# Convolution chain with a Haar layer: the filter networks on 128 partitions, two layers ahead of the first batch, the third inside it

## The chip, the cores and the metric

The kernel runs on one core of a Trainium2 chip (trn2). The metric is the device time in microseconds (us) of one execution. A core has a matrix engine (TensorE, PE in the profile, with its weight loads shown apart as PEld), a vector engine (VectorE, DVE), a scalar engine (ScalarE, ACT), GpSimd (POOL) and SyncE (SP); SP and ACT issue the DMAs here.

## The reference

The input x has 4 batches of 64 channels of 256 x 256 in float32. Four layers follow each other; layers 0, 1 and 3 are long convolutions, layer 2 works in a Haar basis.

```
def filter(z, w1, b1, w2, b2, w3, b3, wo, freq, t, deltas):   # for X and for Y
    h = sin(freq * (z @ w1 + b1)); h = sin(freq * (h @ w2 + b2)); h = sin(freq * (h @ w3 + b3))
    return (h @ wo) * exp(-t * abs(deltas))

# layers 0, 1, 3: k[c] = outer(hx[c], hy[c]); causal 2-d convolution, then the residual
y = irfft2(rfft2(x, 512x512) * rfft2(k, 512x512) / 512)[:256, :256] + x * bias

# layer 2: f = haar2d(x); f4 = conv_w[i] applied over channels to f * v[i]
#          acc += sign(f4) * relu(abs(f4) - tau[i]) for i = 0, 1;  y = haar2d_inverse(acc) + x
```

The kernel of each convolution is an outer product, so the convolution is a product with a triangular Toeplitz matrix along the rows and one along the columns. What the filter networks have to supply is one row of 256 numbers for each channel, axis (X or Y) and layer.

## The kernel before

**The filters (L55 to L138).** All inputs are loaded first. SP issues the Haar matrix `hbt`, `hrow`, the mixing weights `wb`, the biases `bsb`, the signs, the decay table `dsb`, and then for each of the three layers `z` (positions and first weights, 33 partitions) and `w` (the other weights, 64 partitions) (L63 to L93). ACT issues the Haar coefficients `vts` and their factors `fac` (L82 to L85). Then three steps run over the six pairs of a layer and an axis (L97 to L122). One step of one pair is one product of TensorE into 64 x 256 of PSUM (L103 or L105), eight operations of DVE on 64 partitions x 256 (L110 adds the bias and scales, L115 and L116 find the multiple of 2 pi, L118 takes it off in three pieces, L119 clamps) and one Sin on ACT (L121). A last product (L126) and one DVE operation with the decay (L129) give `f`, which L132 writes to the DRAM tensor `pad` of its layer. At the end DVE multiplies the coefficients by their factors (L134), and L135 writes them to the DRAM tensor `scales`.

**The stream of the convolutions.** `toeplitz` (L155 to L159) reads a channel's row from `pad` as 128 shifted copies, 256 KB for the two axes, into one of five buffers `t`. `first` and `second` do the two products of a convolution, each by `contract` (L164 to L168: two products of 256 columns and two of 128). ACT copies the result of the first (L176), DVE adds the residual to that of the second (L189). In batch 0, a channel passes these stages one tick after the other: load of `x` and of layer 0's `t`; `first` of layer 0; `second` of layer 0, which also issues the load of layer 1's `t`; `first` of layer 1; `second` of layer 1 with the first level of the Haar transform (L230, L231) and the write to `keep` (L232). Every four channels DVE does the other levels (L240, L241), and PE does one product each for the other direction (`down`, L259). Then come `mixing` (L284 to L349), which uses `scales` and `wb`, and `inverse` with layer 3's convolution. Batches overlap: the mixing of one runs beside the convolutions of the next.

**The order.** Each stage is put down by `at(tick, place, ...)`, and the list is worked off sorted by tick and place at the end of the function. That fixes the priority of the instructions, but not their order on an engine: a planner with its own cost model places each instruction on its engine's queue when its inputs and a buffer are ready by its reckoning, the lowest in the list first, and so lets later instructions move into gaps. The order on a queue is then fixed in the program, and each engine works its queue off in that order.

Of the kernel before, what the change touches and what calls it, by code (L numbers as in the profile page):

```python
# [9 lines left out]
F32 = mybir.dt.float32  # L10
F32R = mybir.dt.float32r
AF = mybir.ActivationFunctionType
ALU = mybir.AluOpType
PSUM = bass.MemoryType.PSUM
DRAM = bass.MemoryType.DRAM

B, C, S, EMB, ORD = 4, 64, 256, 33, 64
P = 128
ROW = S + P

GT = 8
BUFS = {"res": 1, "y": 3, "co": 2}

INV_2PI = float(np.float32(1.0 / (2.0 * math.pi)))
MAGIC = float(1.5 * 2.0**23)

C1 = 6.28125
C2 = 2028.0 / 2.0**20
C3 = float(np.float32(2.0 * math.pi - C1 - C2))
PI_IN = float(np.nextafter(np.float32(math.pi), np.float32(0)))  # L30


def ap(t, offset, dims):
    return bass.AP(tensor=t.tensor, offset=t.offset + offset, ap=dims)
# [3 lines left out]
def conv_seq_kernel(ctx, tc, x, fz, fw, bias, decay, haar, haar_row, factors, vt, taut, wmix, out):  # L38
# [14 lines left out]
    nc = tc.nc  # L53

    const = ctx.enter_context(tc.tile_pool(name="const", bufs=1))  # L55
    dram = ctx.enter_context(tc.tile_pool(name="dram", bufs=1, space=DRAM))


    hbt = const.tile([P, P], F32, name="hbt")
    hb = const.tile([P, P], F32R, name="hb")  # L60
    hbr = const.tile([P, P], F32R, name="hbr")
    hrow = const.tile([P, 2, P], F32, name="hrow")
    nc.sync.dma_start(hbt, haar[0])  # L63
    nc.sync.dma_start(hrow, haar_row)
    hsinv, ident = hrow[:, 0, :], hrow[:, 1, :]
    wb = const.tile([P, 2, P], F32, name="wb")
    nc.vector.memset(wb, 0.0)
    for r in range(2):
        nc.sync.dma_start(wb[r * C : (r + 1) * C, r, :], wmix)
    bsb = const.tile([P, 3, C], F32, name="bsb")  # L70
    nc.sync.dma_start(bsb, ap(bias, 0, [[0, P], [C, 3], [1, C]]))


    scales = dram.tile([S // 4 // GT, P, 2, GT, 16], F32, name="scales")
    pads = [dram.tile([C, 2, ROW], F32, name=f"pad{layer}") for layer in range(3)]
    with tc.tile_pool(name="filt", bufs=2) as fp, tc.tile_pool(name="fps", bufs=4, space=PSUM) as fps:
        signs = fp.tile([P, P], F32, name="signs", bufs=1)
        nc.sync.dma_start(signs, haar[1])
        nc.scalar.copy(hb, signs)
        nc.scalar.copy(hbr, hbt)  # L80
        vts = fp.tile([P, 2, S // 4, 16], F32, name="vts", bufs=1)
        nc.scalar.dma_start(vts[:, 0], vt)  # L82
        nc.scalar.dma_start(vts[:, 1], taut)
        fac = fp.tile([P, 2, S // 4, 16], F32, name="fac", bufs=1)
        nc.scalar.dma_start(fac, factors)  # L85
        dsb = fp.tile([C, S], F32, name="dsb", bufs=1)
        nc.sync.dma_start(dsb, decay)
        zs, ws = [], []
        for layer in range(3):
            z = fp.tile([EMB, S + 2 * ORD], F32, name=f"z{layer}", tag="z", bufs=3)  # L90
            nc.sync.dma_start(z, fz[layer])
            w = fp.tile([ORD, 2, 3 * ORD + 4], F32, name=f"w{layer}", tag="w", bufs=3)
            nc.sync.dma_start(w, fw[layer])  # L93
            zs.append(z)
            ws.append(w)
        cur = {}
        both = [(layer, axis) for layer in range(3) for axis in range(2)]  # L97
        for step in range(3):
            for layer, axis in both:
                z, w = zs[layer], ws[layer]  # L100
                ps = fps.tile([ORD, S], F32, name=f"fp{step}_{layer}_{axis}", tag="fps")
                if step == 0:
                    nc.tensor.matmul(ps, z[:, S + axis * ORD : S + (axis + 1) * ORD], z[:, :S], start=True, stop=True)  # L103
                else:
                    nc.tensor.matmul(  # L105
                        ps, w[:, axis, (step - 1) * ORD : step * ORD], cur[layer, axis], start=True, stop=True
                    )
                par = 3 * ORD
                u = fp.tile([ORD, S], F32, name=f"u{step}_{layer}_{axis}", tag="u", bufs=3)
                nc.vector.tensor_scalar(  # L110
                    u, ps, w[:, axis, par + step : par + step + 1], w[:, axis, par + 3 : par + 4], ALU.add, ALU.mult
                )

                k = fp.tile([ORD, S], F32, name=f"k{step}_{layer}_{axis}", tag="k", bufs=3)
                nc.vector.tensor_scalar(k, u, INV_2PI, MAGIC, ALU.mult, ALU.add)  # L115
                nc.vector.tensor_scalar(k, k, -MAGIC, None, ALU.add)  # L116
                for c in (C1, C2, C3):
                    nc.vector.scalar_tensor_tensor(u, k, -c, u, ALU.mult, ALU.add)  # L118
                nc.vector.tensor_scalar(u, u, PI_IN, -PI_IN, ALU.min, ALU.max)  # L119
                h = fp.tile([ORD, S], F32, name=f"h{step}_{layer}_{axis}", tag="h", bufs=12)  # L120
                nc.scalar.activation(h, u, AF.Sin)  # L121
                cur[layer, axis] = h  # L122
        for layer, axis in both:
            w = ws[layer]
            ps = fps.tile([C, S], F32, name=f"fo_{layer}_{axis}", tag="fps")
            nc.tensor.matmul(ps, w[:, axis, 2 * ORD : 3 * ORD], cur[layer, axis], start=True, stop=True)  # L126
            f = fp.tile([C, ROW], F32, name=f"f_{layer}_{axis}", tag="f")
            nc.vector.memset(f[:, S:], 0.0)
            nc.vector.scalar_tensor_tensor(  # L129
                f[:, :S], ps, 1.0 / (2 * S) if axis == 0 else 1.0, dsb, ALU.mult, ALU.mult  # L130
            )
            nc.sync.dma_start(pads[layer][:, axis, :], f)  # L132
        for i in range(2):
            nc.vector.tensor_mul(vts[:, i], vts[:, i], fac[:, i])  # L134
            nc.sync.dma_start(  # L135
                scales[:, :, i].rearrange("n p g j -> p n (g j)"), vts[:, i].rearrange("p (n g) j -> p n (g j)", g=GT)
            )


    zpool = ctx.enter_context(tc.tile_pool(name="zpool", bufs=1))  # L140
    tp = ctx.enter_context(tc.tile_pool(name="toep", bufs=5))
    io = ctx.enter_context(tc.tile_pool(name="io", bufs=2))
# [2 lines left out]
    psx = ctx.enter_context(tc.tile_pool(name="psx", bufs=2, space=PSUM))  # L145


    z = zpool.tile([P, 2, S, C], F32, name="z")

    sd = zpool.tile([P, 8, 2, 2, P], F32, name="sd")  # L150
    keep = [dram.tile([C, P, 2, 2, P], F32, name=f"keep{b}") for b in range(B)]
    coef = [dram.tile([2, C, P, S], F32, name=f"coef{b}") for b in range(B)]
    late = dram.tile([B, C, P, 2, S], F32, name="late")

    def toeplitz(layer, c, name):  # L155

        t = tp.tile([P, 2, S], F32, name=name, tag="toep")
        nc.sync.dma_start(t, ap(pads[layer], c * 2 * ROW, [[1, P], [ROW, 2], [1, S]]))
        return t  # L159
# [267 lines left out]


    put_off = range(2, C, 3)
    groups = S // 4  # L430
    ready = convolutions(0, range(C), in_parts=True)
    ahead = C
    start = ready + 3
    for b in range(B):
        mixing(b, start, 8 if b + 1 < B else 6)
        end = start + groups + 3
# [8 lines left out]
        start = max(end + C, ready + 3)  # L445
# [39 lines left out]
def _decay():  # L485
    t = np.linspace(0.0, 1.0, S)
    deltas = np.linspace(math.log(0.01) / 1.5, math.log(0.01) / 0.3, C)
    return np.exp(-t[None, :] * np.abs(deltas)[:, None]).astype(np.float32)[:, ::-1].copy()


# [68 lines left out]
```

## Time and profile before

| | us |
|---|---|
| median of 3 runs | 3088.14 |
| fastest and slowest of them | 3085.73, 3089.94 |
| the profiled execution | 3091.79 |
| its span in the profile | 3090.0 |

| stretch of the span | PE busy | DVE busy | ACT busy | DMA share |
|---|---|---|---|---|
| 8.30 to 57.57 us | 22.95 of 49.27 | 42.06 | 8.73 | 0.31 |
| 57.57 to 66.44 us | 8.18 of 8.87 | 0.75 | 0.59 | 0.54 |
| 66.44 to 345 us | 278.56 of 278.56 | 185.82 | 100.91 | 0.77 |

The profile shows one execution. Its page gives busy times of each engine over the whole span and in 40 slices; other views give the same for chosen stretches, the instructions in order of time (start, duration, engine, line, operation, output and input tiles, and in brackets the idle time before them and what ended it), and the waits by engine and line. PE counts as busy while a product is in its pipeline. The granted clock of TensorE is 1.00 in nearly all stretches.

### The profile page before, as it was taken

How to read it: one execution, taken by the hardware profiler on the slowest of the kernel's cores; microseconds unless marked ns; L12 is line 12 of the kernel's file. 1: busy time of each engine (PE TensorE's matmuls, PEld its weight loads, DVE VectorE, ACT ScalarE, POOL GpSimd, SP SyncE). 2: the span in 40 equal slices, each digit the busy share in tenths (PEclk: the TensorE clock that was granted, in tenths of full speed). 3: DMA queues.
4: the chain of work that ended last, by engine and by line, in shares of the span. 5: the costliest groups of instructions: out<-in, count | busy, mean ns of one | idle time of the engine just before them, and what ended most of it. 6: DMA issues, size and time to landing. Idle time of an engine off the chain costs nothing. (4 is left out here: it accounts for less than half of the span.)

```text
span 3090.0 us, 50474 instructions
## 1 busy us (share of the span) xinstructions
PE 3004.4 (97%) x16944; PEld 2615.3 (85%) x16944; DVE 2523.4 (82%) x4453; ACT 1926.9 (62%) x4054; POOL 0.2 (0%) x4
## 2 busy tenths in 40 slices
PE   5999999999999999999999999999999999999999
PEld 3999988888888888888887888888887888888998
DVE  6667677999987878888886879888886889998776
ACT  1333336777765656667665656666774667887554
POOL 0000000000000000000000000000000000000000
PEclk9999999999999999999999999999999999999999
DMA  4777877666667876666667776666667777877676
GB/s 118 217 230 230 234 227 211 196 193 197 195 193 228 238 223 196 195 207 199 194 205 216 236 229 196 199 195 204 198 195 218 235 238 228 236 233 212 210 211 188
DMA packets 555573, 649.26 MB, mean 210 GB/s; under 512 B 39761, under 2 KB 440500, under 8 KB 555188
## 3 DMA queue, kind: packets, MB, share of 16 engines
q1 hardware_dynamic: 439316, 493.18, 56.5%
q10 hardware_dynamic: 116000, 152.87, 13.7%
q8 instruction: 136, 2.23, 0.3%
q14 instruction: 121, 0.99, 0.1%
HBM read 426.40 MB, written 219.48 MB: 209 GB/s over the span
## 5 line engine op out<-in xcount | busy, mean ns | idle before, releaser
L167 PE MATMUL py<-t,a 128*128 128x256 f32 x3072 | 926.0, 383 | 27.9 <-ACT a L176 24.6
L176 ACT COPY a<-pa 128x512 f32<-128x512 f32 x768 | 458.7, 597 | 466.3 <-PE pa L168 330.7
L168 PEld LDWEIGHTS py<-t,a 128*128 128x128 f32 x3072 | 584.1, 190 | 79.4
L327 ACT ACTIVATE f<-px,vt 128x64 f32<-128x64 f32 x1920 | 422.0, 329 | 352.7 <-DVE f L325 348.3
L167 PEld LDWEIGHTS py<-t,a 128*128 128x128 f32 x3072 | 488.4, 191 | 126.1 <-issue 63.2
L168 PE MATMUL py<-t,a 128*128 128x128 f32 x3072 | 590.6, 274 | 0.0
L308 PE MATMUL px<-wb,f 128*128 128x256 f32 x2048 | 494.2, 380 | 4.3 <-ACT f L327 4.3
L308 PEld LDWEIGHTS px<-wb,f 128*128 128x128 f32 x2048 | 366.0, 191 | 44.1 <-ACT f L327 6.7
L335 DVE TENSOR_TENSOR mag<-mag,vt 128x1024 f32<-128x1024 f32 x256 | 312.2, 1219 | 36.0 <-ACT mag L333 34.8
L167 PE MATMUL pa<-t,x 128*128 128x256 f32 x1024 | 307.5, 382 | 9.4 <-DMA t<-pad 9.3
L340 DVE SCALAR_TENSOR_TENSOR mag<-mag,f 128x1024 f32<-128x1024 f32 x256 | 311.4, 1216 | 0.3
L167 PE MATMUL pa<-t,y 128*128 128x256 f32 x1024 | 306.3, 381 | 1.2 <-DVE y L189 0.9
L333 ACT ACTIVATE mag<-f 128x1024 f32<-128x1024 f32 x256 | 283.9, 1109 | 12.6 <-DVE z L344 6.8
L361 ACT COPY zc<-z 128x512 f32<-128x512 f32 x256 | 281.9, 1102 | 3.9 <-DVE z L199 2.6
L371 ACT CAST w<-pw 128x512 fp32r<-128x512 f32 x256 | 150.2, 587 | 212.3 <-PE pw L369 201.3
L334 ACT ACTIVATE f<-f 128x1024 f32<-128x1024 f32 x256 | 272.0, 1062 | 9.7 <-DVE sd L231 2.4
L189 DVE SCALAR_TENSOR_TENSOR y<-y,bsb,py 128x512 f32<-128x512 f32 x256 | 190.1, 743 | 104.5 <-PE py L168 103.7
L385 DVE SCALAR_TENSOR_TENSOR t<-r,pu 128x512 f32<-128x512 f32 x256 | 175.3, 685 | 86.6 <-PE pu L381 79.6
L189 DVE SCALAR_TENSOR_TENSOR y<-x,bsb,py 128x512 f32<-128x512 f32 x256 | 190.1, 743 | 62.6 <-PE py L168 54.0
L167 PE MATMUL pa<-t,u 128*128 128x256 f32 x772 | 234.1, 385 | 1.1 <-DVE y L189 0.7
L189 DVE SCALAR_TENSOR_TENSOR y<-u,bsb,py 128x512 f32<-128x512 f32 x193 | 143.8, 745 | 102.4 <-PE py L168 98.7
L168 PEld LDWEIGHTS pa<-t,x 128*128 128x128 f32 x1024 | 195.7, 191 | 26.9
(65 smaller groups left out, 4370.7 us busy)
## 6 DMA issues: line engine op xcount, KB each, us to landing
t<-pad SPq DMA_DIRECT2D x768, 256.0 KB, 3.9
x<-in_x SPq DMA_DIRECT2D x256, 256.0 KB, 3.9
keep<-sd ACTq DMA_DIRECT2D x256, 256.0 KB, 3.3
coef<-co SPq DMA_DIRECT2D x256, 256.0 KB, 3.1
f<-coef SPq DMA_DIRECT2D x256, 256.0 KB, 3.9
r<-keep SPq DMA_DIRECT2D x256, 256.0 KB, 3.4
out_y<-y ACTq DMA_DIRECT2D x256, 256.0 KB, 3.6
late<-u ACTq DMA_DIRECT2D x63, 256.0 KB, 2.6
```

The source lines that it names most:

```text
L167: nc.tensor.matmul(ps[:, m, :], src[:, 0, m * P : (m + 1) * P], t[:, ::-1], start=True, stop=False)
L168: nc.tensor.matmul(ps[:, m, P:], src[:, 1, m * P : (m + 1) * P], t[:, : P - 1 : -1], start=False, stop=True)
L176: nc.scalar.copy(a, ps)
L189: nc.vector.scalar_tensor_tensor(y, s[res], bsb[:, layer, c : c + 1], ps, ALU.mult, ALU.add)
L308: nc.tensor.matmul(ps[:, h, q, :], f[:, q, h * P : (h + 1) * P], wb.rearrange("p r n -> p (r n)"), start=True, stop=True,)
L327: nc.scalar.mul(f4[:, j], px[:, j], scale(g, 0)[:, j : j + 1])
L333: nc.scalar.activation(mag, f4, AF.Abs)
L334: nc.scalar.activation(f4, f4, AF.Sign)
L335: nc.vector.tensor_sub(mag, mag, over(g, 1, 16))
L340: nc.vector.scalar_tensor_tensor(mag, mag, 0.0, st[g]["f4"], ALU.max, ALU.mult)
L361: nc.scalar.copy(a, z[:, :, :, c].rearrange("p h (i k) -> p h k i", k=2))
L385: nc.vector.scalar_tensor_tensor(t, st[c]["r"], 0.5, ps, ALU.mult, ALU.add)
```

## The change

Four things change.

The whole block L59 to L138 goes; what it did is put elsewhere. The six pairs become three units: `filters(layer, queue)` works the X and the Y axis of one layer together on 128 partitions, with block diagonal weights made on the host (128 x 388 for one layer), so that one step is one product 128 x 256, eight DVE operations 128 x 256 and one Sin. The scale 1/512 of the X axis comes from a column of `dsb`. The two halves of `f` go to `pad` by two DMAs, on ACT's and on SP's queue.

Only layers 0 and 1 stand ahead of the convolutions, interleaved by hand, layer 0 first. The Haar constants (`constants`), layer 3's filter (`three`) and the coefficients (`tables`) are put into the list as stages of their own at place 3, the last place of a tick: constants at tick 4, layer 3's load at 7, its steps at 8 to 13, its end at 14, the load of the coefficients at 15 and the two scalings with their writes at 16 and 17. Their DMAs are on SP's queue, but for one half of `f`.

`warm(n)` adds products without use: 128 x 256, from `f` on itself into a PSUM tile nobody reads, six after layer 0's end and nine after layer 1's end.

All work tiles of the filters lie in the space of `z` (128 KB on each partition), which the kernel first writes in the mixing of batch 0. The coefficients lie over layer 0's and layer 1's inputs and over part of layer 3's.

```
...
-        both = [(layer, axis) for layer in range(3) for axis in range(2)]
-        for step in range(3):
-            for layer, axis in both:
...
+    room = z.rearrange("p h r c -> p (h r c)")
+    def filters(layer, queue):
+        fz_sb, fw_sb = part(S + P, EMB), part(3 * P + 4)
...
+        def load():
+            nc.sync.dma_start(fz_sb, fz[layer])
+            queue.dma_start(fw_sb, fw[layer])
+        def begin(n):
+            ps = bank(f"fp{layer}_{n}").rearrange("p m s -> p (m s)")[:, :S]
...
+            u, k = st["u"], st["k"] = part(S), part(S)
...
+            nc.vector.tensor_scalar(k, k, -MAGIC, None, ALU.add)
+        def finish(n):
+            u, k, h = st["u"], st["k"], part(S)
+            for c in (C1, C2, C3):
+                nc.vector.scalar_tensor_tensor(u, k, -c, u, ALU.mult, ALU.add)
+            nc.vector.tensor_scalar(u, u, PI_IN, -PI_IN, ALU.min, ALU.max)
+            nc.scalar.activation(h, u, AF.Sin)
...
+        def end():
...
+            nc.tensor.matmul(ps, fw_sb[:, 2 * P : 3 * P], st["h"], start=True, stop=True)
+            nc.vector.scalar_tensor_tensor(f[:, :S], ps, dsb[:, S:], dsb[:, :S], ALU.mult, ALU.mult)
+            for axis, queue in enumerate((nc.scalar, nc.sync)):
+                queue.dma_start(pads[layer][:, axis, :], f[axis * C : (axis + 1) * C])
+        def warm(n):
+            ps = psx.tile([P, 2, S], F32, name=f"warm{layer}", tag="mix")
+            for i in range(n):
+                nc.tensor.matmul(ps[:, i % 2, :], st["f"][:, :P], st["f"][:, :S], start=True, stop=True)
+        steps = [(lambda n=n, do=do: do(n)) for n in range(3) for do in (begin, finish)]
+        return [load, *steps, end, warm]
...
+    def tables():
...
+        def load():
+            nc.sync.dma_start(vts[:, 0], vt)
+            nc.sync.dma_start(vts[:, 1], taut)
+            nc.sync.dma_start(fac, factors)
...
+    one, two, three = filters(0, nc.scalar), filters(1, nc.scalar), filters(2, nc.sync)
+    one[0]()
+    nc.sync.dma_start(dsb, decay)
+    two[0]()
+    nc.sync.dma_start(bsb, ap(bias, 0, [[0, P], [C, 3], [1, C]]))
+    for do in (one[1], one[2], two[1], one[3], one[4], two[2], one[5], one[6], two[3], one[7], *two[4:7]):
+        do()
+    one[8](6)
+    two[7]()
+    two[8](9)
+    for tick, do in enumerate([constants, None, None, *three[:-1], *tables()], 4):
+        if do is not None:
+            at(tick, 3, lambda unit, do=do: do(), 0)
```

## The prediction

> **What bounds the kernel now.** I read the page first (busy shares, 40 slices), then the busy times by stretches of 10 us, the instructions in order of time up to 80 us, and last the waits and the DMA issues.
>
> ```profile
> PE 3004.4 (97%) x16944; PEld 2615.3 (85%) x16944; DVE 2523.4 (82%) x4453; ACT 1926.9 (62%) x4054; POOL 0.2 (0%) x4
> ...
> PE   5999999999999999999999999999999999999999
> ```
>
> TensorE is full in all slices but the first, so the gap to look into is there. The stretches (length, then PE, PEld, DVE, ACT, POOL busy, granted clock, DMA share, GB/s):
>
> ```profile
> 40.00:50.00 10.00, 4.87 (x11) 1.42 (x10) 10.00 (x30) 1.67 (x4) 0.00 (x0) 1.00 0.12 29
> 50.00:60.00 10.00, 2.41 (x7) 2.08 (x8) 1.57 (x7) 0.00 (x0) 0.00 (x0) 1.00 0.90 245
> 60.00:70.00 10.00, 9.33 (x40) 8.03 (x39) 1.37 (x2) 1.76 (x3) 0.00 (x0) 1.00 0.38 102
> 70.00:80.00 10.00, 10.00 (x62) 9.19 (x62) 4.03 (x9) 2.35 (x4) 0.00 (x0) 1.00 0.67 188
> ```
>
> Up to 47 us DVE is the bound (10.00 of 10.00), then DMA (0.90), then PE for good. The instructions (start, duration, engine, line, operation):
>
> ```profile
> 8.33 5.38 PE L103 MATMUL fp<-z 33*64 33x256 f32 x12 [8.33 <-DMA z<-in_fz]
> 8.73 2.22 SPq L221 DMA_DIRECT2D x<-in_x  x4
> 9.48 0.53 DVE L110 TENSOR_SCALAR u<-fp,w 64x256 f32<-64x256 f32 x1 [8.08 <-PE fp L103]
> ...
> 13.38 0.42 ACT L121 ACTIVATE h<-u 64x256 f32<-64x256 f32 x1 [3.85 <-DVE u L119]
> 14.21 0.29 PEld L105 LDWEIGHTS fp<-h,w 64*64 64x64 f32 x2 [1.33 <-ACT h L121]
> ...
> 46.64 0.41 DVE L129 SCALAR_TENSOR_TENSOR f<-fo,dsb 64x256 f32<-64x256 f32 x1
> 47.08 1.12 SPq L132 DMA_DIRECT2D pad<-f  x2
> 48.74 1.51 SPq L135 DMA_DIRECT2D scales<-vts  x2
> 52.64 1.09 SPq L158 DMA_DIRECT2D t<-pad  x2
> 53.97 0.34 SPq L294 DMA_DIRECT2D vt<-scales  x1
> 57.59 1.19 PE L167 MATMUL pa<-t,x 128*128 128x256 f32 x2 [8.46 <-DMA t<-pad]
> 61.16 1.22 PE L167 MATMUL py<-t,a 128*128 128x256 f32 x2 [0.67 <-ACT a L176]
> 66.44 0.71 PE L167 MATMUL pa<-t,y 128*128 128x256 f32 x2
> ```
>
> The first convolution starts at 57.59. Three contractions run until 66.44 (those starting at 57.59, 61.16 and 63.88), each some 2.55 us; from 66.44 on one takes 1.31 (the next start at 67.76 and 69.07). So the state at 66.44 is that of a start at full speed at 66.44 - 3 x 1.31 = 62.5. I use the event "first product of layer 1 (`pa<-t,y`)" as the marker: from 66.44 to 345 us PE is busy 278.56 of 278.56, so whatever moves this event moves the batch.
>
> **What the skill says.** (1) The Trainium skill, "VectorE: DVE Perf Modes", section "The TRN2 errata": an fp32 tensor_tensor costs (N+151)/0.96 ns, N being the elements on a partition; partitions don't enter. For N = 256 that is 424 ns; L230 on 128 x 256 shows 424, L118 on 64 x 256 shows 409. (2) "TensorE: Matmul & The Clock Gate", Part 1: a cold array runs at half rate until about 3.4 us of sustained activity. The trace agrees with the half (2.55 against 1.31), though the switch came 8.8 us after 57.59 with a wait of 0.67 between, and the granted clock says 1.00 all along. (3) "DMA: Bandwidth & Descriptors", "Queues, rings and completion order": what one engine issues goes through its own rings in order, on the same 16 DMA engines as the other's. So a large load on SP delays the `t` behind it; the 256 KB `t` take 3.9 us in the median of the run and 4.8 between 40 and 70 us, beside the `scales`.
>
> **The change, part by part** (all against the span of 3090.0 us).
>
> Start. `z` is issued at 5.08 on SP, behind seven other DMAs, and used at 8.33: 3.25 us. Issued first, at 0.73, it is used at 3.98. `w` goes on ACT's queue at 0.73; its 198 KB against 98 (2.8 us to landing) may bring it 1 us later, still before DVE asks for it at 5.1. One table load of 1.28 us is hidden in that wait.
>
> DVE. In place of 18 rounds of eight operations there are 6 before the convolutions, at the same duration each (1). A lone round: product to DVE 1.15 (8.33 to 9.48); 0.53 + 3 x 0.28 + 3 x 0.41 = 2.60, with 0.03 between dependent operations 2.75; Sin 0.42; ACT to the next weight load 0.41 (13.80 to 14.21): 4.75 in all. Layer 0: 3.98 + 3 x 4.75 + 1.15 + 0.41 = 19.8 for its `f`, where before had the first at 47.05. The last rounds of layer 1 lie behind: its second round's DVE part starts after layer 0's third (17.4), ends with layer 0's end between at 20.6; two passes through ACT and PE (1.98 each), one DVE part and the end give 27.7. The work tiles start at odd element offsets in `z`; if that cost the three SBUF-only operations their 0.28 against 0.41, it would be 0.13 x 9 = 1.2 on this path. Nothing shows it: bound 0 to 1.2, I take 0.
>
> To the convolutions. Layer 1's `pad` lands 3.0 us after 27.7 (median), its `t` 3.9 later: 34.6. PE: six products without use fill gaps after 20; the nine stand after 27.7. A 256-column product is a third of a contraction: 0.85 cold, 0.44 warm, so they end between 31.7 and 35.4. The three contractions after them take 3.9 warm and 0.7 to 1 of waiting for ACT, as at 60.5. The marker falls at 36.4 to 40.2, later than the `t` needs; I take 37.8. **Gain: 66.44 - 37.8 = 28.6**, bounds 26 to 32 (32 if the planner lets the contractions run ahead of the nine, and the `t` at 34.6 decides).
>
> Layer 3, constants. PE: four products at 0.44 = 1.75 when among the convolutions, nothing if the planner pulls them ahead as it pulled the four `x` loads (8.73) and a `vt` (53.97): 1.0, bounds 0 to 1.75. DVE: three rounds at 2.06 (half the 4.13 from 13.61 to 17.74 for two), an end, 2 x 1.2 for the coefficients: 9 us, in a stretch where DVE has a third free. What queues behind them on DVE is the residual `y` (L189), for which PE waits two contractions later (2.6 us, less 0.75): a round's second half (1.5) just fits. On ACT three Sin and two casts, 1.9 us, in front of the copies that PE awaits, with about as much room. If these pieces are pulled forward they sit between layer 1's rounds instead. Cost 1.0, bounds 0 to 3.
>
> Coefficients. 2 MB of loads and 1 MB of writes, formerly beside the filters (first 10 us) and beside `pad` and `t` (48 to 57), go to SP's queue among the convolutions, where DMA is 0.77 busy. Six `t` are wanted at once and there are five buffers, so a `t` is issued when PE frees one. Layer 1's is freed one contraction into a tick (1.31), lands 3.9 later (5.2) and is needed one contraction into the next tick (4 x 1.31 + 1.31 = 6.55): room 1.3 us, and the same for layer 0's. Behind 1.5 to 2 MB at the 290 GB/s reached around 53 us a `t` loses 5 to 7 us; behind a 512 KB write 1.8. Stall: from 0 (pulled to where PE waits anyway, or split by the planner) to (7 - 1.3) + 2 x (1.8 + 1.2 - 1.3) = 9. I take 4.
>
> Sum: 28.6 - 1.0 - 1.0 - 4.0 = 22.6. The profiled execution (3091.79, span 3090.0) lies 3.7 above the median of 3088.14; I take the gain off the median: **3065.5**.
>
> **Rivals.**
> A. The coefficients are free: they move under layer 1's wait, where DMA was 0.00 to 0.12 busy in the filter stage. For it: the planner does pull loads ahead. Against: they lie over layer 3's inputs. Gain 28.6 less 0 to 2, a little more if their DMAs leave `pad` and `t` alone: some 29, 3059.
> B. SP stands still: scaling and write follow the load on SP's queue, and every `t` behind waits for DVE. Load 7, multiply 1.2, twice a write 1.8, 1.2 more: 13 less 1.3; 28.6 - 2 - 12 = 14.6, 3073.5. For it: SP's waits for buffers, 949 us on L158 in total.
> C. Slower: the eleven stages at ticks 4 to 17 each hold PE, because the planner puts a DMA or a round in front of the `t` or the `y` that PE wants next. At 4 us a stage it is 44 - 28.6 = +15, 3103.5; it decides from 28.6/11 = 2.6 a stage. Against it: room of 1.3 to 1.9 us each.
> D. The useless products don't hold the clock: the wait between them and layer 1's `t` is long enough for a cold start. Three contractions at 2.55 in place of 1.31: 3.7, so 3069. It lies within my forecast's range.
>
> **How the numbers follow.** Forecast with D 0.60 (3060 to 3071), A 0.15, B 0.17, C 0.04; 0.04 for a loss elsewhere (the mixing stages replanned) that eats the gain without more. The range takes in A and B but for their outer parts: 3055 to 3080. Faster by over 0.2% (6.2 us, about what a measurement of this kernel can tell from no change): 0.92; within: 0.04; slower: 0.04.
>
> **What would show it.** First filter product near 4.0; first `f` near 19.8, layer 1's near 27.7; contractions of 1.31 from their start; `pa<-t,y` near 37.8. Waits of PE for `t<-pad` behind the coefficients' loads, some 4 us in all, tell forecast from A and B. A marker after 42, or PE idle over 10 us between it and 345 - 28 us, would make it wrong; so would mixing stages that differ from before by more than the shift.

## The result and the profile after

| | before | after |
|---|---|---|
| median of 4 runs each | 3086.93 us | 3070.60 us |
| fastest and slowest | 3083.40, 3089.94 | 3068.05, 3078.94 |
| span of the profiled execution | 3090.0 | 3066.3 |
| ratio after to before | | 0.9952, 95% interval 0.9930 to 0.9974 |

The changed kernel is faster by 16.3 us between the medians (8 to 22 by the interval) and by 23.7 between the two profiled spans. A second, larger set of runs of the same kernel (the first experiment) gave 18.4 us, ratio 0.9941 with an interval of 0.9928 to 0.9953. The forecast was 22.6 us, to 3065.5.

The top of the page of the changed kernel (busy us, share, instructions; then tenths busy in 40 slices):

```profile
PE 2998.0 (98%) x16950; PEld 2618.5 (85%) x16950; DVE 2505.8 (82%) x4384; ACT 1919.6 (63%) x4044; POOL 0.2 (0%) x4
...
PE   7999999999999999999999999999999999999999
```

Only the first slice has changed, from 5 to 7: most of what is gained lies in the first 77 us. The busy times of its first stretches (length, PE, PEld, DVE, ACT, POOL, granted clock, DMA share, GB/s):

```profile
10.00:20.00 10.00, 2.94 (x6) 1.32 (x5) 6.81 (x21) 1.23 (x4) 0.00 (x0) 1.00 0.06 20
...
40.00:50.00 10.00, 10.00 (x63) 9.23 (x62) 4.29 (x8) 2.34 (x4) 0.00 (x0) 1.00 0.60 180
...
60.00:70.00 10.00, 9.88 (x57) 8.55 (x56) 6.11 (x12) 1.82 (x4) 0.00 (x0) 1.00 0.55 170
```

While the filters of layers 0 and 1 run, DVE no longer fills a stretch (6.81 of 10.00 where it was 10.00 up to 47 us). PE fills the stretch from 40 us on, where before the first full one began at 70. But in the last line PE has 9.88, and from 110 to 120 us only 8.05, where before it never left 10.00 from 70 us on. The instructions in order of time:

```profile
3.17 1.22 PE L109 MATMUL fp<-z 33*128 33x256 f32 x2 [3.17 <-DMA z<-in_fz]
...
9.64 1.22 PE L111 MATMUL fp<-z 128*128 128x256 f32 x2 [3.57 <-ACT z L125]
14.33 2.08 PE L111 MATMUL fp<-z 128*128 128x256 f32 x4 [3.46 <-ACT z L125]
20.52 1.22 PE L130 MATMUL fo<-z 128*128 128x256 f32 x2 [4.11 <-ACT z L125]
21.78 0.48 DVE L133 SCALAR_TENSOR_TENSOR z<-fo,z 128x256 f32<-128x256 f32 x1 [1.56 <-PE fo L130]
22.38 4.70 PE L142 MATMUL warm<-z 128*128 128x256 f32 x12
27.55 0.49 DVE L133 SCALAR_TENSOR_TENSOR z<-fo,z 128x256 f32<-128x256 f32 x1 [1.29 <-PE fo L130]
28.09 4.15 PE L142 MATMUL warm<-z 128*128 128x256 f32 x18 [0.58 <-DVE z L133]
32.08 0.59 PE L189 MATMUL pa<-t,x 128*128 128x256 f32 x2
32.51 0.38 PE L190 MATMUL pa<-t,x 128*128 128x128 f32 x2
...
36.95 0.60 PE L189 MATMUL pa<-t,y 128*128 128x256 f32 x2
```

Layer 0's filter is there at 22.26 (start and duration of the first L133), layer 1's at 28.04. The first convolution stands directly behind the nine useless products of 28.09, with no wait of its own. The marker `pa<-t,y` falls at 36.95 in place of 66.44: 29.5 us. Not all of it is kept. PE's two largest waits in the 110 us behind the marker (total us, times, longest), of 3.7 us in all, where before had none:

```profile
PE pa L189 <- DMA t<-pad: 1.5, 1, 1.5
PE pa L189 <- DVE y L211: 1.2, 3, 0.5
```

**A second ruler.** DVE adds the residual 768 times (L189 before, L211 after), in the same order in all kernels, so the start of the same residual in two profiles says by how much one kernel is ahead there. At the 49th residual (200.43 and 178.74 us, when layer 3's filter and the coefficients are done) the changed kernel is 21.7 us ahead, at the last one 24.1. So the loss behind the marker is 29.5 - 21.7 = 7.8 us; a further gain of 2.4 comes much later. All kernels on this ruler:

| kernel | marker at | ahead at the marker | ahead at residual 49 | loss between | ahead at the last | median of the times |
|---|---|---|---|---|---|---|
| before | 66.44 | 0 | 0 | 0 | 0 | 3086.9 to 3088.6 |
| after | 36.95 | 29.5 | 21.7 | 7.8 | 24.1 | 3070.6 |
| after, repeated | 36.73 | 29.7 | 24.2 | 5.5 | 19.6 | 3070.2 |
| no useless products | 35.62 | 30.8 | 25.0 | 5.9 | 27.2 | 3064.6 |
| six useless products only | 34.30 | 32.1 | 25.1 | 7.1 | 35.4 | 3054.2 |
| coefficients apart | 38.52 | 27.9 | 25.9 | 2.0 | 23.1 | 3067.4 |
| all three layers first | 42.87 | 23.6 | 23.6 | 0.0 | 22.5 | 3069.9 |
| coefficients in pieces | 37.06 | 29.4 | 25.8 | 3.6 | 30.4 | 3061.9 |
| 64 partitions | 54.28 | 12.2 | 2.1 | 10.1 | 11.2 | 3080.5 |
| layers in turn | 38.65 | 27.8 | 20.5 | 7.3 | 29.4 | 3062.8 |
| in turn, eight useless products | 35.11 to 35.22 | 31.2 to 31.3 | 24.5 to 25.0 | 6.2 to 6.8 | 32.0 to 35.1 | 3055.1, 3059.3, 3057.2 |
| the same, coefficients in pieces | 33.54 | 32.9 | 26.4 | 6.5 | 37.2 | 3053.6 |

The columns up to the residual 49 can be followed in the trace. What lies between it and the last residual is a subject of its own, at the end of the next section.

### The profile page after: what moved, and what is told of

It is laid out like the page before. It is cut to its first block, busy times and chain, and to the rows that moved or that the text cites. A ratio compares the mean times of both kernels' runs of the same rounds, so it can differ in the third digit from the quotient of the medians.

```text
span 3066.3 us, 50357 instructions
## 1 busy us (share of the span) xinstructions
PE 2998.0 (98%) x16950; PEld 2618.5 (85%) x16950; DVE 2505.8 (82%) x4384; ACT 1919.6 (63%) x4044; POOL 0.2 (0%) x4
## 5 line engine op out<-in xcount | busy, mean ns | idle before, releaser
L189 PE MATMUL py<-t,a 128*128 128x256 f32 x3072 | 925.5, 383 | 30.4 <-ACT a L198 26.2
L189 PEld LDWEIGHTS py<-t,a 128*128 128x128 f32 x3072 | 488.1, 191 | 128.7 <-issue 64.0
L189 PE MATMUL pa<-t,y 128*128 128x256 f32 x1024 | 306.9, 381 | 2.7 <-DVE y L211 2.3
L189 PE MATMUL pa<-t,x 128*128 128x256 f32 x1024 | 305.8, 380 | 1.7 <-DMA t<-pad 1.5
L356 ACT ACTIVATE f<-f 128x1024 f32<-128x1024 f32 x256 | 272.1, 1063 | 10.1 <-DVE sd L253 3.7
L211 DVE SCALAR_TENSOR_TENSOR y<-y,bsb,py 128x512 f32<-128x512 f32 x256 | 190.3, 743 | 101.8 <-PE py L190 101.0
L211 DVE SCALAR_TENSOR_TENSOR y<-x,bsb,py 128x512 f32<-128x512 f32 x256 | 190.4, 744 | 57.7 <-PE py L190 49.3
L189 PE MATMUL pa<-t,u 128*128 128x256 f32 x772 | 234.4, 385 | 0.6 <-DVE u L411 0.5
L211 DVE SCALAR_TENSOR_TENSOR y<-u,bsb,py 128x512 f32<-128x512 f32 x193 | 143.9, 746 | 99.8 <-PE py L190 98.1
L262 DVE TENSOR_TENSOR sd<-sd 128x512 f32<-128x512 f32 (+6 forms) x448 | 164.3, 367 | 65.8 <-DMA keep<-sd 38.0
```

What stands on the lines that cost most here:

```text
L189: nc.tensor.matmul(ps[:, m, :], src[:, 0, m * P : (m + 1) * P], t[:, ::-1], start=True, stop=False)
L211: nc.vector.scalar_tensor_tensor(y, s[res], bsb[:, layer, c : c + 1], ps, ALU.mult, ALU.add)
L356: nc.scalar.activation(f4, f4, AF.Sign)
```

## The experiments

My theory after the result was: of the 7.8 us lost behind the marker, the coefficients' DMAs take the larger part and layer 3's four products the rest; and the nine useless products stand in front of the convolutions rather than help them. The rivals: the overlap of batches was planned anew and costs something; layer 3's rounds on DVE delay the residuals; without useless products three contractions run cold.

**1. The changed kernel once more.**

> The changed kernel once more, to narrow its ratio. If the single profiled execution tells the gain (span 3066.3 against 3090.0, 23.7 us), the ratio comes near 0.992; if the four runs' medians do (3070.6 against 3086.9, 16.3 us), near 0.995. First product of layer 1 at 37.0 us, PE idle some 3.7 us between 57 and 147 us.

Measured: 3070.18 us (3066.94 to 3072.86), span 3070.7. The ratio of 0.9941 lies between the two cases, nearer to that of the medians. The marker is at 36.73, so the start repeats to 0.2 us; the loss up to residual 49 is 5.5 in place of 7.8, and PE waits 2.2 us in the 110 us behind the marker, not 3.7. A single profile therefore fixes the cost behind the marker only to some 2 us.

**2. No useless products.**

```diff
-    one[8](6)
     two[7]()
-    two[8](9)
```

> The changed kernel without the fifteen products without use. If they earn their place: the first convolution starts about 2.5 us earlier (29.5) but cold, three contractions of 2.55 us, first product of layer 1 near 38.2, so 1 us slower than the changed kernel. Rival, the nine only hold the convolutions back: contractions are at 1.31 us soon, first product of layer 1 near 34.5, 2.5 us faster.

Measured: 3064.59 us, ratio 0.9921 (0.9908 to 0.9935), faster than the changed kernel beside it (experiment 1) by 5.6. The instructions in order of time:

```profile
29.32 1.19 PE L189 MATMUL pa<-t,x 128*128 128x256 f32 x2 [2.12 <-issue]
...
30.73 1.06 PE L189 MATMUL pa<-t,x 128*128 128x256 f32 x2
...
32.90 0.70 PE L189 MATMUL py<-t,a 128*128 128x256 f32 x2 [0.68 <-ACT a L198]
```

The first `t` is used at 29.32, 2.8 us ahead of the 32.08 above. Only the first contraction is cold (1.06 where 0.60 is full rate), the second is already at full rate at 32.90. So the fifteen useless products as they stand lose 1.3 us at the marker; 35.62 is nearer to the rival's 34.5 than to 38.2. In the two traces, PE's order differs by these fifteen products alone, and DVE's (4384 instructions) and SP's not at all; on ACT only a few neighbours change places. Against the kernel before, the orders on PE, DVE and SP differ only in the filters and the first part of batch 0. The rival of batches planned anew is refuted by that.

**3. The coefficients in a stretch of `z` of their own**, so that nothing holds back their loads.

```diff
-        free[0] = S + 1
+        free[0] = 16384
...
+        free[0] = S + 1 + 4096
```

> The coefficients lie in a stretch of their own in z, so that nothing holds their loads back and the planner can pull them ahead of the convolutions; all else as changed. Theory, their loads behind tick 15 cost the 1.5 us wait of PE for the t and about 0.7 us of waits for y: PE idle between 57 and 147 us falls from 3.7 to about 1.5, first product of layer 1 stays at 37 to 38, span 2 us shorter. Rival, their 3 MB only move the stall: in front of the first pads and t, first product of layer 1 at 40 or later, span equal or longer.

Measured: 3067.4 us, ratio 0.9930 (0.9917 to 0.9942). PE has no wait at all in the 110 us behind the marker, and the loss is 2.0. Layer 3's filter still runs among the convolutions here: it costs its products and next to nothing else. The coefficients, then, cost 5.8 us in the profile of the result and 3.5 in its repetition, if layer 3 costs the same in all three. But the marker is at 38.52. In order of time:

```profile
21.55 1.51 SPq L172 DMA_DIRECT2D scales<-z  x2
...
26.94 0.81 SPq L317 DMA_DIRECT2D vt<-scales  x2
...
29.26 8.50 SPq L181 DMA_DIRECT2D t<-pad  x6
33.55 0.70 PE L190 MATMUL pa<-t,x 128*128 128x256 f32 x2 [0.68 <-DMA t<-pad]
```

The pulled-forward writes of `scales` and the reads of `vt` stand in front of `pad` and `t` on SP, and the first `t` is issued at 29.26 where the changed kernel issues it at 26.06. So 1.6 us of the cost has moved in front of the marker (1.8 against the repetition). At residual 49 this kernel is still 1.7 to 4.2 us ahead of the changed one, and in the median 2.8 us ahead of the one beside it, where the intervals of the ratio overlap. What was measured lies between theory and rival.

**4. All three layers in turn ahead of the convolutions**, coefficients apart as in 3.

```diff
+    three[0]()
...
-    for do in (one[1], one[2], two[1], one[3], one[4], two[2], one[5], one[6], two[3], one[7], *two[4:7]):
-        do()
-    one[8](6)
+    for step in range(1, 7):
+        for layer in (one, two, three):
+            layer[step]()
+    one[7]()
     two[7]()
+    three[7]()
+    one[8](6)
     two[8](9)
...
```

> As tables_apart, and all three layers' filters ahead of the convolutions, step by step in turn. Theory, the gain comes from the 128 partitions and from the gaps in DVE that a third chain fills: nine rounds at 2.06 us end near 25.5, layer 1's pad leaves near 26 to 28 as in the changed kernel, first product of layer 1 near 37.5, and behind it PE has no idle time and no products of layer 3 (5.4 us less), span near 3061. Rival, moving layer 3 behind is what gains: with it ahead the first product of layer 1 comes at 37 + 3 x 2.06 = 43 and the span is 3067 to 3070.

Measured: 3069.85 us, ratio 0.9938 (0.9924 to 0.9951). The loss behind the marker is nil, as it must be with nothing left there, but the marker is 5.4 us later than my theory had it, and where the rival had it (42.87 for 43; the span of 3067.9 is in its range too):

```profile
19.33 8.50 SPq L173 DMA_DIRECT2D scales<-z  x2
...
28.19 3.95 SPq L135 DMA_DIRECT2D pad<-z  x3
30.94 7.22 PE L142 MATMUL warm<-z 128*128 128x256 f32 x26
...
32.87 2.47 SPq L182 DMA_DIRECT2D t<-pad  x5
38.00 0.59 PE L191 MATMUL pa<-t,x 128*128 128x256 f32 x2
```

Layer 0's filter, in turn with two others, ends 5.9 us later than in the changed kernel (28.17). Three `pad` writes on SP take until 32.1, so the first `t` is issued at 32.87, and thirteen useless products keep PE until 38.0. Against experiment 3 the marker is 4.4 us later and the loss 2.0 smaller: at residual 49 it is worth 2.3 us to have layer 3 behind the convolutions' start. The times say the same (2.5 us), with intervals that overlap.

**5. Units of 64 partitions again**, everything else as in the changed kernel (two layers first, useless products, layer 3 in the ticks). Each axis is a unit with its own tiles:

```diff
-        fz_sb, fw_sb = part(S + P, EMB), part(3 * P + 4)
+        fz_sb, fws = part(S + P, EMB), [part(3 * P + 4, C) for _ in range(2)]
...
+        units = [unit(axis) for axis in range(2)]
         def begin(n):
+            for u in units:
+                u[0](n)
```

> The changed kernel with its filters back on 64 partitions, one unit for each axis; order, placing and useless products as changed. Theory: DVE then has twelve rounds of 2.06 us ahead of the convolutions, 4.4 + 24.7 + 2.4 = 31.5 for layer 1's last f in place of 27.6, first product of layer 1 near 41; four products of layer 3 more among the convolutions (1.75 us); span 6 to 8 us longer than the changed kernel. Rival, the 128 partitions are most of the gain: each of six more rounds counts in full, first product of layer 1 at 37 + 12.4 = 49, span 14 us longer.

Measured: 3080.51 us over 9 runs, ratio 0.9976 (0.9966 to 0.9985). The marker is at 54.28, where my theory had 41 and its rival 49: both too early. In order of time:

```profile
37.37 1.22 PE L210 MATMUL pa<-t,x 128*128 128x256 f32 x2
37.48 0.42 DVE L136 SCALAR_TENSOR_TENSOR z<-fo,z 64x256 f32<-64x256 f32 x1 [0.44 <-PE fo L133]
38.52 8.05 PE L163 MATMUL warm<-z 64*128 64x256 f32 x18
46.50 0.80 PE L211 MATMUL pa<-t,x 128*128 128x128 f32 x2
...
54.28 0.60 PE L210 MATMUL pa<-t,y 128*128 128x256 f32 x2
```

Layer 1's filter ends at 37.90, 9.9 us behind the changed kernel: that is what the 128 partitions give to the filters themselves. Another 3.9 us is the nine useless products, which take 8.05 in place of 4.15: they run cold. They stand between the first product of layer 0's first convolution and the rest of it. And from 46.50 to the marker it takes 7.8 us, where the changed kernel takes 4.4 from the same product (32.51): the contractions are cold too. 9.9 + 3.9 + 3.4 = 17.2 of the 17.3 us at the marker. Of the 29.5 us, then, 12.2 come with all the rest of the change at the old width (two layers in place of three, their order, the start of the loads), and 17.3 with the width and what follows from it.

**6. The coefficients in eight pieces**, stages at ticks 15 to 30, each loading or scaling one eighth.

```diff
-        def load():
-            nc.sync.dma_start(vts[:, 0], vt)
...
+        def load(n):
+            g = slice(n * GT, (n + 1) * GT)
+            nc.sync.dma_start(vts[:, 0, g], vt[:, g])
...
+        def scale(n):
...
+            nc.vector.tensor_mul(vts[:, :, g], vts[:, :, g], fac[:, :, g])
+            nc.sync.dma_start(scales[n], vts[:, :, g])
```

> The changed kernel with the coefficients loaded, scaled and written in eight pieces (256 KB in, 128 KB out), still in the stages from tick 15 on. Theory, a single large load in front of a t on SP's rings is what PE waits for: PE idle in the 110 us behind the first product of layer 1 falls from 2.2 to 3.7 to under 1, first product of layer 1 stays near 37, span 2 to 3 us shorter. Rival, the bytes count and not their grouping: the same idle time, spread over more ticks.

Measured: 3061.9 us, ratio 0.9918 (0.9905 to 0.9932). The marker is unchanged (37.06), and the loss behind it is 3.6 us in place of 5.5 and 7.8. All waits of PE in the 110 us behind the marker:

```profile
PE pa L189 <- DVE y L211: 0.8, 1, 0.8
PE pz L281 <- DVE y L211: 0.3, 1, 0.3
```

No wait for `t` is left. That repeats: the changed kernel and experiments 1, 2, 7, 8, 9, 11 and 12, all with whole tables, have one such wait each, of 1.5 to 2.2 us, and the two kernels with pieces (6 and 10) have none. So large transfers in front of a `t` make PE wait for it, and small ones don't. That pieces lower the whole loss is not shown: 3.6 is within some 2 us of 5.5, and experiment 10 has no smaller loss than its kernel with whole tables.

**7. and 8. Layers 0 and 1 step by step in turn**, without useless products and with eight of them behind both ends.

```diff
-    for do in (one[1], one[2], two[1], one[3], one[4], two[2], one[5], one[6], two[3], one[7], *two[4:7]):
-        do()
-    one[8](6)
-    two[7]()
-    two[8](9)
+    for step in range(1, 8):
+        one[step]()
+        two[step]()
+    one[8](8)
```

(The last line is in experiment 8 alone.)

> No useless products, and the first two layers step by step in turn in place of layer 0 first. Theory, layer 1's second product stands behind layer 0's third on PE and its chain leaves DVE idle; in turn both are done near 22.5 us (21.8 and 27.6 before). The first convolution still starts near 29.3 behind layer 0's pad and t, one contraction runs cold: first product of layer 1 near 35.6, as in no_warm. Rival: layer 1's t was what it waited for, and it comes 5 us earlier, near 31.

> As turns, with eight products without use behind both layers' last products, in the 7 us in which PE waits for pad and t. Theory: they end before 29.3, hold nothing back, and all three contractions run at 1.31: first product of layer 1 near 33.9, 1.7 us before turns. Rival: as in the changed kernel they end later than the t lands, or the clock falls back before the convolutions: 35.6 or later.

Measured: 3062.77 us without (ratio 0.9920, 0.9907 to 0.9934) and 3055.1 with the eight (0.9896, 0.9882 to 0.9909). In order of time behind the two filters, first without, then with:

```profile
29.89 1.19 PE L189 MATMUL pa<-t,x 128*128 128x256 f32 x2 [6.92 <-DMA t<-pad]
...
37.47 1.06 PE L189 MATMUL pa<-t,x 128*128 128x256 f32 x2
...
38.65 0.60 PE L189 MATMUL pa<-t,y 128*128 128x256 f32 x2
```

```profile
22.72 5.34 PE L142 MATMUL warm<-z 128*128 128x256 f32 x16
30.13 0.70 PE L189 MATMUL pa<-t,x 128*128 128x256 f32 x2 [2.08 <-DMA t<-pad]
...
35.11 0.60 PE L189 MATMUL pa<-t,y 128*128 128x256 f32 x2
```

In turn, both filters end by 23.5, so the second is there 4.5 us sooner than in the changed kernel. The first `t` comes to PE no sooner (29.89), since layer 0's filter ends no sooner (22.64 against 22.26). Without useless products all three contractions are cold, until 38.5, where I had expected one and the marker at 35.6. The eight useless products end 2.1 us ahead of the first `t`, delay nothing, and the convolutions start at full rate: the marker is 3.5 us earlier, though 1.2 later than the theory's 33.9. Useless products do what they are meant to do where they end before the data is there.

**9. and 10. Kernel 8 again, and kernel 8 with the coefficients in pieces** (the edits of 8 and 6 together).

> The kernel with the two layers in turn and eight useless products, once more, on the chip and in the call of the next one. If its 3055.1 us belong to the program and not to the call, it is within 4 us of that, the marker at 35.1 within 0.3, PE idle in the 110 us after it 3 us. If a good part of its gain over the changed kernel (15 us in the times against 2 us at the marker) was luck with the half-rate windows of TensorE's clock, it falls between 3060 and 3066.

> The two layers in turn, eight useless products, and the coefficients in eight pieces instead of three whole tables. Theory (the 3 us of PE idle in the first batch come from the large DMAs of the coefficients alone, and add to the rest): marker 35 as without the pieces, idle after it at most 1, the time 2 to 3 us under that of the kernel with whole tables in this call. Rival (pieces pulled forward stand in front of layer 1's pads and their copies on SP): marker 36.5 or later, and no difference in the time.

Measured: 3059.29 us (0.9916, 0.9902 to 0.9929) and 3053.60 (0.9889, 0.9875 to 0.9902). The times differ by 5.7, more than I expected, but the trace gives only part of that: the marker is 1.6 us earlier (33.54), and the loss behind it is the same 6.2 to 6.5, with another cause: there is no wait for `t` any more, but 3.0 us of waits for the residual on DVE. So the theory was right on the waits for `t` and wrong on what is left without them; the 3059.3 lies just outside the 4 us that I had allowed it and under the 3060 of the other case.

**11. and 12. Six useless products only, and kernel 8 a third time beside it.**

```diff
     one[8](6)
     two[7]()
-    two[8](9)
```

> As the changed kernel, without the nine useless products behind layer 1's end; the six behind layer 0's end stay. Theory (the six alone bring the clock up, since they and layer 1's last product end 2 us before the first t has landed; the nine only stand in front of the convolutions): first convolution at 29.3 as without useless products, at 0.44 us a product and not 0.85, marker at 33.9 to 34.5 if layer 1's t (issued at 30.6) is there, at most 35 if not; PE idle after the marker 2.2 to 3.7 as in the changed kernel; the time 2 to 3 us under it, near 3067 if the times follow the trace. Rival (the clock falls back in the 2 us without work): first contraction cold, marker 35.6, the same as without useless products. Side question: the kernel without useless products came out 5.6 us under the changed one in the times, 1.1 us of it at the marker; if that gap belongs to the nine products, this one comes out at 3064 or less.

> The kernel with the two layers in turn and eight useless products, beside the kernel with six useless products in the changed kernel's order. Both have the same queue orders from the first convolutions on. If only the marker counts, it is within 1.5 us of the other. If something later in the program gains by the order in turn, it is 5 us or more below the other, though the orders are the same.

Measured: 3054.22 us (0.9887, 0.9870 to 0.9903) and 3057.15 (0.9900, 0.9885 to 0.9915). Kernel 11 in order of time:

```profile
22.27 4.54 PE L142 MATMUL warm<-z 128*128 128x256 f32 x12
...
29.11 0.70 PE L189 MATMUL pa<-t,x 128*128 128x256 f32 x2 [1.87 <-DMA t<-pad]
...
34.30 0.67 PE L189 MATMUL pa<-t,y 128*128 128x256 f32 x2
```

The first contraction starts with the `t` (29.11) and at full rate, although PE waited 1.87 us before it: the clock is held by the six. The marker of 34.30 is within what the theory gave (33.9 to 34.5), 2.65 us ahead of the changed kernel: that is what the nine cost. The kernel in turn is 2.9 us slower beside it, 0.9 of it at the marker: the order in turn gains nothing later. The time of 3054.2 is far below the 3064 that I had set as the sign that the gap of 5.6 us in experiment 2 belongs to the nine products, and 16 us below the changed kernel: much more than the nine cost at the marker. Kernels 10 and 11 are the fastest of the study (3053.6 and 3054.2, intervals of the ratio overlap); 11 differs from the changed kernel by one line left out.

**What stays open: the stretch from residual 49 to the last.** Kernel 11 gains 2.65 us on the changed kernel at the marker and 3.4 at residual 49, but 11.4 at the last residual and 16 in the times. The orders in its trace are those of the changed kernel but for nine products, so nothing that it does later is different. The table shows that the kernels fall into two sorts here: 5 and 7 to 12 get a further 8 to 11 us ahead of the kernel before behind residual 49, kernels 1 to 4 and the changed one between -5 and +2, and kernel 6 stands between them with 5. The repeated kernels stay in their sort (8, 9 and 12; the changed one and 1), and so do the times (3065 to 3071 in the second sort, 3054 to 3063 in the first but for the 64 partitions), so it is not one profile's luck. Between kernel 11 and the changed one it builds up from 4.3 us at 764 us to 11.1 at 2351 us, where batches overlap. PE's largest wait from 760 to 2340 us (total, times, longest), changed kernel and then kernel 11; the next one is 4.2 us in both:

```profile
PE py L189 <- ACT a L198: 16.1, 20, 1.7
```

```profile
PE py L189 <- ACT a L198: 11.5, 17, 1.4
```

The copies `a` come late a few times more often, 4.6 us in all of the 6.8 by which the two drift apart there; the granted clock (0.91 in one stretch of 20 us in both) is no part of the difference. Neither the place of the marker (34.3 and 54.3 in one sort, 35.6 and 66.4 in the other) nor the number of instructions sorts the kernels. One thing does, but for kernel 6: kernels 1 to 4 ran on one chip, and 5 to 8, 9 and 10, 11 and 12 on three others. The kernel before took 3088.6, 3087.5, 3088.3 and 3088.6 us on the four, so none of the four is faster with that kernel. But the changed kernel is on record for the first of them alone (experiment 1; its first runs name no chip), so it stays open whether the program or the chip decides the course. Times of kernels 5 to 12 set against those of the changed kernel (the 16 us of kernel 11, the 8 us of kernel 6) compare different chips; the changed kernel and kernel 11 on one chip would tell. So the 13 us that kernel 11 is better beyond its marker are measured and not explained.

## Why the prediction was right, and where it was off

The direction, the place and the forecast case were right; 3070.6 is 5.1 us above the predicted time, inside the range.

- **Start.** Predicted 3.98 for the first product; it was 3.17.
- **DVE, layer 0.** A round has seven operations on DVE (L113, L117, L118, three of L123, L124), not the eight that the description of the kernels counts; the prediction's 2.60 is the sum of seven. Predicted 19.8 for its filter, measured 22.26: 3.3 us too short from the true start. The lone round of 4.75 was right where a round was alone (9.64 to 14.33: 4.69). The other two took 6.5 (3.17 to 9.64) and 6.2 (14.33 to 20.52), because operations of layer 1 stand between layer 0's on DVE. I had counted them only on layer 1's path.
- **DVE, layer 1.** Predicted 27.7, measured 28.04. This is in part luck: the path began 0.8 us earlier than predicted and took some 1.1 us longer.
- **Useless products and marker.** Predicted end between 31.7 and 35.4, measured 32.2; marker 37.8 predicted (36.4 to 40.2), 36.95 measured. That the marker would come "later than the `t` needs" is confirmed by kernel 11: by 2.65 us.
- **Layer 3 and constants.** Predicted 1.0 + 1.0. With the coefficients out of the way (experiment 3) the loss is 2.0; with layer 3 ahead too (experiment 4) it is 0.0. The split between PE and DVE was not right: PE had no wait in experiment 3, so all of it was PE's own time. The planner pulled only loads ahead.
- **Coefficients.** Predicted 4.0 in bounds of 0 to 9; 5.8 and 3.5 in the two profiles. In the profile of the result, waits that name `t` are only 1.5 us of the 5.8 and waits for DVE 1.9. The rest, some 2 us, stands in no wait: PE counts as busy in it, with ends that the profile models, and what takes it is not shown.
- **The sum.** 28.6 - 6.0 was predicted for a point where 29.5 - 7.8 = 21.7 was measured and 24.2 in the repetition: 22.6 lies between, closer than the scatter of 2 us between two profiles of one kernel would let one claim. The step to the time is the mis-sized one: it took a gain in the first batch for a gain at the end, and the overlapped batches move a time by -5 to +11 us behind it. With the repetition, the times gave 16 to 18 us.

**The rivals.** A, free coefficients: only one `vt` load was pulled forward in the changed kernel; where all could be (experiment 3), they cost 1.6 us of marker instead, and the time was 3067.4, not 3059. B, SP standing still, showed in small. In order of time, around the scaling of the changed kernel:

```profile
104.76 0.34 SPq L167 DMA_DIRECT2D z<-in_factors  x1
...
107.18 2.38 SPq L180 DMA_DIRECT2D t<-pad  x2
113.50 1.23 DVE L170 TENSOR_TENSOR z<-z 128x1024 f32<-128x1024 f32 x1 [4.06 <-DMA keep<-sd]
114.76 0.36 SPq L171 DMA_DIRECT2D scales<-z  x1
...
115.82 0.67 PE L189 MATMUL pa<-t,x 128*128 128x256 f32 x2 [1.46 <-DMA t<-pad]
115.84 1.13 SPq L180 DMA_DIRECT2D t<-pad  x1
```

From 109.6 to 114.76 SP issues nothing, then the write that waited for DVE, and the next `t` only at 115.84; PE waits once for the `t` issued behind the factors. The cost of all of it was 5.8 in the costlier of the two profiles, where B asked for some 12. C, eleven stages that hold PE, did not come: all eleven cost 7.8 us, 0.7 a stage. D, a clock that falls back: false for the changed kernel, whose first contraction takes full rate; experiments 5 and 7 show that its price was about right (3.4 and 3.5 us). The Trainium skill, "TensorE: Matmul & The Clock Gate", Part 1, has a busy window of some 3.4 us before full rate: experiment 2 agrees (3.6 us, 29.32 to 32.90), experiment 7 does not (8.6 us, 29.89 to 38.5, with one wait of 0.67 between), so the measurement decides: this start may take one contraction or three. The same part calls the window free-running and the number of cold products different from run to run, so experiment 2 may have been lucky with its window; PE had also paused for 2.12 us before its first convolution and for 6.92 in experiment 7. No run here parts the two.

## What to carry to other kernels

When a start-up is shortened, price three things apart: how early the first dependent event of the bound engine comes, what the moved work takes behind it, and what the same DMAs do on the queue if they are pulled forward instead; in experiment 3, removing 3.5 to 5.8 us behind the event cost 1.6 to 1.8 in front of it. Filler work that holds a clock must end before the awaited data lands; one line too many of it cost 2.65 us here, and one that ends 2 us early cost nothing. Compare kernels at matched instructions (the n-th residual) and not by the end time alone, since here the end moved by up to 11 us more, for reasons that stayed open; and run the kernels to be compared on one chip.

## What the runs showed of the hardware that was not expected

**Half-rate windows in the middle of the run.** In 12 of the 14 profiles the granted clock falls to half once or twice in the middle, near 945, 1650 to 1675 or 2350 us, for 3.41 us each. In the changed kernel (same columns as above):

```profile
945.00:950.00 5.00, 2.62 (x8) 1.68 (x8) 2.21 (x10) 1.17 (x2) 0.00 (x0) 0.78 0.39 119
950.00:952.00 2.00, 2.00 (x10) 1.76 (x9) 0.66 (x2) 1.46 (x2) 0.00 (x0) 0.70 0.40 135
```

PE had paused for 2.38 us from 945.08 on, and the record has the low clock from 947.8. All 15 such falls come within 3.8 us of the start of a pause of 1.9 to 3.4 us; a pause of 2.2 us in kernel 11 (at 110 us) brought none. The loss is 5.00 x 0.22 + 2.00 x 0.30 = 1.7 us of full clock. The repetition of the same kernel had two such windows, kernel 10 none between 740 and 2360 us; so they come and go between executions of one program.

**A cold start of two lengths.** The page and the stretches give a granted clock of 1.00 while contractions take twice their time (experiments 2, 5 and 7, and before up to 66 us). But the record of the clock in these traces begins only later, and what lies ahead of it is counted as 1.00: it begins at 32.7 us in experiment 2, 38.5 in experiment 7, 54.0 in experiment 5, 66.7 before and 26.2 in the changed kernel, each time within some 0.3 us of the first products at full rate where these can be seen. So a 1.00 there says nothing, and the beginning of the record does; the duration of a 128 x 256 product shows the state too (1.06 against 0.60 as recorded). The useless products of experiment 5, on 64 rows, ran 8 us at the cold rate without ending it.
